# Attention and mixture-of-experts kernel: one transfer for the layernorm statistics, gate biases on GpSimd's queue, results read a tile sooner, four late stores on other queues or places

## The chip, the cores and the metric

The kernel runs on one core of a Trainium2 chip. The core has five engines that run at the same time: TensorE (PE, matrix products), VectorE (DVE), ScalarE (ACT), GpSimd (POOL) and SyncE (SP). SyncE, ScalarE and GpSimd each have a queue from which they issue transfers; 16 DMA engines, shared by all queues, move the data between the main memory (DRAM) and the on-chip memory (SBUF). Matrix products land in PSUM, which is read by VectorE and ScalarE.

The metric is the device time in microseconds (us). Three runs of the kernel before gave 610.34, 611.74 and 612.23; the median is 611.74. A profile shows one execution, with the start and length of each instruction and with what an engine waited for.

## The reference, cut to what matters

For each of B = 4 batches of 512 tokens with 512 features (1024 context rows), all in float32:

```python
# x: (4, 512, 512), ctx: (4, 1024, 512)
h = layernorm(x)
q, g = h @ Wq.T, sigmoid(h @ Wg.T + bg)
k, v = split(ctx @ Wkv.T)                  # 16 heads of 32
q, k = where(q > 0, q + 1, exp(q)), where(k > 0, k + 1, exp(k))
attn = (q @ (k.T @ v)) / (q @ sum(k) + 1e-6)   # per head
x = x + (attn * g) @ Wo.T
# two of eight experts for each token
h = layernorm(x)
w, sel = top_k(h @ Wr, 2); w = softmax(w)
x = x + sum_i w[i] * (h @ We[sel[i]] + be[sel[i]])
```

## The kernel before, in words

**Attention.** Context tiles of 128 rows (eight a batch) are loaded by `load_ctx` into three buffers (`cT`); `keys` and `values` multiply them by `wkv_sb` into PSUM (`pk`, `pv`), and `kv_add` adds the products of keys and values into `kvs`. `query` and `gate` multiply the transposed, normalized x (`xT`) by `wq_sb` and `wg_sb`; the gate's sigmoid (line 423) takes its bias from `bg_sb`. `products` and `attention_out` finish the attention. The program order on TensorE is kept, by `keep_in_program_order`. So is that of SyncE's loads, all of which go through `load` (line 102): a load that waits for a buffer holds back those behind it.

**The layernorm in front of the attention.** x is also loaded as `blocks` (`load_blocks`), in a layout in which 32 by 32 transposes on VectorE give `xT`. In that layout the rows of a token sit on other partitions than in the tiles on which the statistics are made. `layernorm_stats` makes mean and variance of four tiles of 128 tokens (into `mv`, four pairs a partition) and from the variance 1/sqrt (into `rstd`). `spread_moments` writes both to DRAM (`moments`), by GpSimd's queue, and reads them back four times, into 32 partitions each (`ln`). `normalized_T` uses `ln` as scalars. For batch 0 the order on SyncE's queue is: weights and x, the context tile 3, `wq`, `blocks`, `wr`, context tile 4, then for seven pieces a load of `bg_sb` and one of `wo_sb` in turn (lines 948 to 950), then context tiles 5 and 6. The biases are loaded as columns of single floats.

**The experts.** `choose` picks two experts for each token and `dispatch` scatters the tokens' rows into a DRAM buffer `stream`, sorted by expert (GpSimd's indirect DMAs). `run` goes over tiles of 128 rows of it. There are EARLY = 17 tiles that can be taken before the last batch is sorted, and then SURE = 18 late steps. At step j of `run`, SyncE issues the loads of tile j + 5 (four parts of `xg`, and `of` with the token numbers; line 765), TensorE multiplies tile j by its expert's weights (`pe`), VectorE adds the bias (`y`, line 814), GpSimd scatters y into `result` (line 818), and VectorE transposes tile j + 3 (line 782).

**Reading the results.** The output has 16 tiles of 128 tokens. `fetch` reads both choices of a tile from `result` (`y<-result`, 0.5 MB, line 889), `add` combines them with x on VectorE (line 902), and `store` writes the tile to the output (line 913). A read waits until as many scatters as its group in `READ` asks for have landed: 13 for tiles 0 to 3, 21 for 4 to 7, 26 for 8 and 9, 29 for 10 and 11, 33 for 12 and 13, all for 14 and 15. `begins` gives the late step after which the read of tiles 0 to 13 is placed; the add stands three steps later and the store one more, unless the read begins at step 14 (SURE - 4) or later: then add and store come after the loop. `queue_of` gives GpSimd's queue up to step 12 and ScalarE's after it. On each queue the order is that of the program. After the loop the reads of 14 and 15 go out on ScalarE's queue, then the adds and stores that are left; the store of tile 14 is on SyncE's queue, that of 15 on ScalarE's.

Of the kernel before, what the change touches and what calls it, by code (L numbers as in the profile page):

```python
# [9 lines left out]
F32 = mybir.dt.float32  # L10
I32 = mybir.dt.int32
U32 = mybir.dt.uint32
AF = mybir.ActivationFunctionType
ALU = mybir.AluOpType
# [3 lines left out]
P = 128  # L18
B, L, S, D = 4, 512, 1024, 512
E, F = 8, 512  # L20
HD = 32
NC = D // P
NT = L // P
# [16 lines left out]
SURE = LATE - 4  # L40
# [13 lines left out]
def xattn_moe_kernel(  # L54
# [14 lines left out]
    nc = tc.nc  # L69
# [10 lines left out]
    small = ctx.enter_context(tc.tile_pool(name="small", bufs=2))  # L80
    pmm = ctx.enter_context(tc.tile_pool(name="pmm", bufs=6, space=PSUM))
    pkv = ctx.enter_context(tc.tile_pool(name="pkv", bufs=1, space=PSUM))
    dram = ctx.enter_context(tc.tile_pool(name="dram", bufs=1, space=DRAM))
# [3 lines left out]
    result = dram.tile([NOWHERE + 2 * L, F], F32, name="result")  # L87


    moments = dram.tile([B, HD, NT, P // HD, 2], F32, name="moments")  # L90


    def matmul(**operands):
# [8 lines left out]
    def load(dst, src):  # L102
        latest["load"] = nc.sync.dma_start(out=dst, in_=src)  # L103
        tc.keep_in_program_order(latest["load"])
# [39 lines left out]
    bg_sb = wpool.tile([P, NC], F32, name="bg_sb")  # L144
# [17 lines left out]
    xs = {0: load_x(0)}  # L162

    turned = [(g, 0, g * HD, P - g * HD) for g in range(NC)]
# [17 lines left out]
    eps_sb = const.tile([P, 1], F32, name="eps_sb")  # L182
# [16 lines left out]
    for g in range(NC):  # L199
        r = slice(g * HD, (g + 1) * HD)  # L200
        for i in range(NC):
            o = (i + g) % NC
            nc.gpsimd.affine_select(
                out=spread[r, o, :], in_=spread[r, o, :], pattern=[[0, HD]],
# [49 lines left out]
    def layernorm_stats(tiles):  # L254
        mv = small.tile([P, NT, 2], F32, tag="mv", name="mv")
        for t in range(NT):
            st = small.tile([P, 6], F32, tag="st", name="st")
            nc.vector.bn_stats(st, tiles[t])
            nc.vector.bn_aggr(mv[:, t, :], st)
        rstd = small.tile([P, NT], F32, tag="rstd", name="rstd")  # L260
        nc.scalar.activation(rstd, mv[:, :, 1], AF.Sqrt, bias=eps_sb)
        nc.vector.reciprocal(rstd, rstd)
        return mv, rstd

    def normalize(dst, xt, t, mv, rstd):
        nc.vector.tensor_scalar(
            dst, xt, mv[:, t, 0:1], rstd[:, t : t + 1], ALU.subtract, ALU.mult
        )

    def transposed(dst, src):  # L270

# [4 lines left out]

    def spread_moments(b, tiles):

        mv, rstd = layernorm_stats(tiles)
        for k, of in enumerate((mv[:, :, 0], rstd)):  # L280
            nc.gpsimd.dma_start(
                out=moments[b, :, :, :, k].rearrange("t n j -> j t n"), in_=of
            )
        ln = small.tile([P, NT, P // HD, 2], F32, tag="ln", name="ln", bufs=1)
        for i in range(NC):
            nc.gpsimd.dma_start(
                out=ln[ts(i, HD)].rearrange("t n j k -> t (n j k)"),
                in_=moments[b].rearrange("t n j k -> t (n j k)"),
            )
        return ln  # L290

    def normalized_T(xT, t, blocks, ln):

        rows = blocks[:, ts(t, D)].rearrange("p (j f) -> p j f", f=P)
        with tc.issue_after(latest["map"].ins):
            for j in range(P // HD):
                nc.vector.tensor_scalar(
                    rows[:, j], rows[:, j], ln[:, t, j, 0:1], ln[:, t, j, 1:2],
                    ALU.subtract, ALU.mult,
                )  # L300
            nc.vector.transpose(
                xT[:, :, ts(t, P)].rearrange("p c (j t) -> p j c t", t=HD),
                rows.rearrange("p j (c f) -> p j c f", f=HD),
            )
# [41 lines left out]
    def kv_blocks(psum):  # L346
        for h in range(P // HD):
            r = slice(h * HD, (h + 1) * HD)
            nc.scalar.copy(h_kv[r], psum[r, :, r])
            nc.vector.tensor_copy(h_ks[r, :, h : h + 1], psum[r, :, P : P + 1])  # L350
# [23 lines left out]
    def kv_tiles(b, lo, hi, between=None, inside=None):  # L374
        for s in range(lo, hi):
            nxt = (b, s + 2) if s + 2 < NS else (b + 1, s + 2 - NS)
            if nxt[0] < B and nxt not in loaded_ctx:
                loaded_ctx.add(nxt)
                ctx_tiles[nxt] = load_ctx(*nxt)
            if b in (1, 2) and s % 2 == 0:  # L380
                e = (b - 1) * E // 2 + s // 2
                for i in range(NC):
                    load(we_sb[ts(i, HD), e], we_rows[e, i])
            for e in (s,) if b else (2 * (s - NS // 2), 2 * (s - NS // 2) + 1):
                if e >= 0:
                    set_empty(b, e)
            if s == 0:
                sums[b] = pkv.tile([P, NC, 2 * P], F32, tag="kvs", name="kvs")
            k = made.pop(s) if s in made else keys(b, s)
            if (b, s) == (0, 0):  # L390
                made[1] = keys(0, 1)
            if inside is not None and s == lo:
                inside()
            v = values(b, s)
            if s > 0:
                kv_add(sums[b], s - 1, *pending[b])
            pending[b] = k, v
            if between is not None:
                between(s - lo)
        if hi == NS:  # L400
            kv_add(sums[b], NS - 1, *pending[b])
# [121 lines left out]

    routed = {}

    def choose(b, mv, rstd):

        rows = []
        batch = work.tile([P, NT, ROW], F32, tag="row", name="rows", bufs=1)
        for t in range(NT):  # L530
            row = batch[:, t, :]
            normalize(row[:, 0:D], xs[b][t], t, mv, rstd)
            nc.gpsimd.tensor_copy(row[:, D : D + 1], home[:, b * NT + t : b * NT + t + 1])
            rows.append(row)

        xT = big.tile([P, NC, L], F32, tag="aT", name="x2T")
        for t in range(NT):
            transposed(xT[:, :, ts(t, P)], rows[t])
            yield

        ps = pmm.tile([P, L], F32, tag="mm", name="ps")
        for c in range(NC):
            matmul(
                out=ps[ts(c, HD), :],
                lhsT=wr_sb[:, c, :],
                rhs=xT[:, c, :],
                start=True,
                stop=True,
                tile_position=(0, c * HD),
            )  # L550
        share = work.tile([P, L], F32, tag="z", name="share")
        nc.scalar.copy(share, ps)
        yield
        pl = pmm.tile([P, NT, E], F32, tag="mm", name="pl")
        for t in range(NT):
            matmul(
                out=pl[:, t, :], lhsT=share[:, ts(t, P)], rhs=by_expert, start=True, stop=True
            )
        lg = small.tile([P, NT, E], F32, tag="lg", name="lg")
        nc.vector.tensor_copy(lg, pl)  # L560

        def largest(name):
            m = small.tile([P, NT, 1], F32, tag=f"m{name}", name=f"m{name}")
            hot = small.tile([P, NT, E], F32, tag=f"hot{name}", name=f"hot{name}")
            at = small.tile([P, NT, 1], F32, tag=f"at{name}", name=f"at{name}")
            nc.vector.tensor_reduce(m, lg, AX.X, ALU.max)
            nc.vector.tensor_tensor(hot, lg, m.to_broadcast([P, NT, E]), ALU.is_equal)
            nc.vector.tensor_tensor(hot, hot, rank, ALU.mult)
            nc.vector.tensor_reduce(at, hot, AX.X, ALU.max)
            nc.vector.tensor_tensor(hot, hot, at.to_broadcast([P, NT, E]), ALU.is_equal)  # L570
            return m, hot, at

        m1, hot1, first = largest("1")
        nc.vector.scalar_tensor_tensor(lg, hot1, -BIG, lg, ALU.mult, ALU.add)
        m2, hot2, _ = largest("2")

        routed[b] = rows, m1, hot1, first, m2, hot2
        yield
# [347 lines left out]
    def plan(step, *what):  # L926
        at_step.setdefault(min(step, SURE), []).append(what)

    def queue_of(step):
        return nc.gpsimd if step < SURE - 5 else nc.scalar  # L930

    begins = (-3, -2, -1, 0, 5, 6, 7, 8, 10, 11, 14, 15, SURE - 2, SURE - 2)
    for g, (lo, hi, most) in enumerate(READ):
        for t in range(lo, hi):
            plan(begins[t], fetch, t, most, queue_of(begins[t]), g)
    for t, begin in enumerate(begins):
        step = begin + (3 if begin < SURE - 4 else SURE)
        plan(step, add, t, gates if step < SURE else gates_end)
        plan(step + 1, store, t, queue_of(step + 1))

    def also(j):
        for what, *of in at_step.pop(j, []):
# [3 lines left out]
    xT = new_xT()  # L946
    kv_tiles(0, 0, 3)
    for g, a, b, n in turned:
        load(bg_sb[b : b + n, g : g + 1], bg[a : a + n, g : g + 1])
        load(wo_sb[b : b + n, g, :], wo[a : a + n, g, :])  # L950
    ln = spread_moments(0, xs[0])

# [2 lines left out]
            normalized_T(xT, t, blocks, ln)  # L955

    kv_tiles(0, 3, NS, between)
    kv_blocks(sums[0])
    for b in range(B):
        more = b + 1 < B  # L960
# [43 lines left out]
        if more:  # L1004
# [11 lines left out]
            ln = []  # L1016
# [4 lines left out]
            for _ in range(3):  # L1021
                next(early)
        attention_out(b, aT)
        choice = choose(b, *layernorm_stats(xs[b]))
        if more:

            def between(i):
# [133 lines left out]
```

## Time and profile before

| what | us |
|---|---|
| median of three runs | 611.74 |
| the profiled execution | 610.59 |
| its span, first to last instruction | 608.9 |
| TensorE busy | 576.7 |
| VectorE busy | 289.6 |
| GpSimd busy | 120.5 |
| ScalarE busy | 109.3 |

Instructions are named by line, engine, operation and "out<-in" with the program's names of tiles. `pk<-wkv_sb,cT` is a matmul of a context tile with the weights of the keys. "SPq", "ACTq" are transfers as they are issued on SyncE's and ScalarE's queues; "x4" stands for four in a row. In a line of the timeline the first number is the start and the second the length, in us; a bracket at the end gives how long the engine had been idle and what ended it. The row PEclk gives the granted clock of TensorE in 40 equal slices, in tenths of full speed (9 is 90% or more). The table by stretch gives start and end, the length, the busy time of PE, its weight loads, DVE, ACT and POOL with the number of instructions, and at the end the clock, the share of time in which the 16 DMA engines are busy (it can exceed 1, as packets overlap), and GB/s.

### The profile page before, as it was taken

To read this page: it belongs to the slowest core of one execution; us is meant where nothing else is said; L and a number is where in the kernel's file an instruction comes from. 1 tells how busy PE (TensorE), PEld (TensorE's weight loads), DVE (VectorE), ACT (ScalarE), POOL (GpSimd) and SP (SyncE) were. 2 spreads that over 40 slices of the span, in tenths; PEclk is the share of its full clock that TensorE was granted. 3 is DMA by queue.
4 is the path that set the end of the run, shared out by engine and by line. 5 is a ranking of instruction groups with operands and counts; after the bars stand their busy time and mean duration, and the time that the engine had idled before them with its cause. 6 is when DMAs were issued, how large, how long until landed. Compare 5 with 4: busy or idle time off the path is not lost.

```text
span 608.9 us, 6440 instructions
## 1 busy us (share of the span) xinstructions
PE 576.7 (95%) x1780; PEld 270.0 (44%) x1780; DVE 289.6 (48%) x732; ACT 109.3 (18%) x168; POOL 120.5 (20%) x289
## 2 busy tenths in 40 slices
PE   7989999999999999999999999999999999998950
PEld 3545544454555435445543454554344443443420
DVE  2215254354317443541564355128765579473863
ACT  1311241220313321122242121221300110000000
POOL 4230021000001510000061100003211237444630
PEclk9989999999999999999999999999999999999995
DMA  8979995374490698627338660952255444889866
GB/s 283 166 122 355 340 197 48 116 238 131 121 277 19 140 240 261 190 87 209 103 140 147 236 203 5 315 221 108 89 119 121 121 122 167 251 235 295 243 225 212
DMA packets 78933, 109.87 MB, mean 180 GB/s; under 512 B 13229, under 2 KB 39853, under 8 KB 78768
## 3 DMA queue, kind: packets, MB, share of 16 engines
q1 hardware_dynamic: 68112, 79.91, 49.0%
q0 software_dynamic: 8336, 24.29, 12.2%
q10 hardware_dynamic: 2448, 5.24, 2.6%
q8 instruction: 15, 0.25, 0.2%
q14 instruction: 22, 0.18, 0.1%
HBM read 50.19 MB, written 59.96 MB: 181 GB/s over the span
## 4 chain that ended last, share of the span: by engine, by line
PE 74%; DMA 9%; DVE 6%; SPq 4%; issue 4%; POOL 1%; DVEq 0%; ACTq 0%; POOLq 0%
PE pk L94 18%; PE pv L94 16%; PE pq L94 9%; PE po L94 9%; PE pg L94 7%; PE pe L94 5%; PE kvs L94 4%; DMA xg<-stream 4%; DMA cT<-in_cT_dram 3%; SPq L765 2%; SPq L103 1%; PE pn L94 1%; PE pt L97 1%; DMA result<-y,to 1%; DMA of<-stream 1%
## 5 line engine op out<-in xcount | busy, mean ns | idle before, releaser
L94 PE MATMUL pk<-wkv_sb,cT 128*128 128x512 f32 x256 | 119.4, 611 | 6.4 <-DMA cT<-in_cT_dram 6.4
L94 PE MATMUL pv<-wkv_sb,cT 128*128 128x512 f32 x256 | 115.2, 593 | 0.0
L250 DVE TENSOR_SCALAR ex<-pk 128x512 f32<-128x512 f32 x32 | 22.1, 692 | 135.1 <-PE pk L94 135.1
L94 PEld LDWEIGHTS pv<-wkv_sb,cT 128*128 128x128 f32 x256 | 48.4, 190 | 62.3 <-issue 59.8
L94 PEld LDWEIGHTS pk<-wkv_sb,cT 128*128 128x128 f32 x256 | 48.0, 196 | 60.9 <-issue 53.4
L94 PE MATMUL pe<-we_sb,xgT 128*128 x144 | 62.8, 594 | 3.9 <-DVE xgT L782 3.9
L94 PE MATMUL pe<-we_sb,turned_rows 128*128 x136 | 60.4, 596 | 1.9 <-DVE turned_rows L782 1.5
L94 PE MATMUL pg<-xT,wg_sb 128*128 128x512 f32 x128 | 56.7, 595 | 0.0
L94 PE MATMUL pq<-xT,wq_sb 128*128 128x512 f32 x128 | 56.6, 596 | 0.0
L94 PE MATMUL po<-wo_sb,aT 128*128 128x512 f32 x128 | 55.6, 592 | 0.0
L818 POOL DMA_INDIRECT result<-y,to x35 | 36.4, 1041 | 94.0 <-DVE y L814 91.3
L251 ACT ACTIVATE ex<-ex 128x512 f32<-128x512 f32 x48 | 30.2, 629 | 137.5 <-DVE ex L250 117.3
L330 POOL MEMSET v<- 128x4 f32 x32 | 3.3, 108 | 245.4 <-PE kvs L94 245.3
L94 PEld LDWEIGHTS pe<-we_sb,xgT 128*128 128x128 f32 x144 | 27.1, 190 | 39.4 <-issue 32.2
L624 POOL DMA_INDIRECT stream<-rows,slot x32 | 32.9, 1027 | 51.7 <-DVE acc L587 22.2
L94 PEld LDWEIGHTS kvs<-v,k 128*128 128x128 f32 x256 | 33.3, 191 | 16.0 <-issue 14.2
L94 PEld LDWEIGHTS pe<-we_sb,turned_rows 128*128 128x128 f32 x136 | 25.2, 190 | 34.0 <-issue 29.9
L94 PEld LDWEIGHTS pg<-xT,wg_sb 128*128 128x128 f32 x128 | 24.0, 190 | 32.1 <-issue 32.1
L94 PEld LDWEIGHTS po<-wo_sb,aT 128*128 128x128 f32 x128 | 24.1, 190 | 29.2 <-issue 28.7
L94 PEld LDWEIGHTS pq<-xT,wq_sb 128*128 128x128 f32 x128 | 23.8, 190 | 27.3 <-issue 27.3
L94 PE MATMUL kvs<-v,k 128*128 128x129 f32 x256 | 34.1, 275 | 0.0
L252 DVE SCALAR_TENSOR_TENSOR k<-pk,ex 128x512 f32<-128x512 f32 x32 | 22.1, 691 | 21.6 <-ACT ex L251 21.6
(183 smaller groups left out, 459.7 us busy)
## 6 DMA issues: line engine op xcount, KB each, us to landing
stream<-empty SPq DMA_DIRECT2D x24, 1028.0 KB
stream<-empty SPq DMA_DIRECT2D x8, 1285.0 KB
xg<-stream SPq DMA_DIRECT2D x140, 64.0 KB
we_sb<-in_we_dram SPq DMA_DIRECT2D x32, 256.0 KB
cT<-in_cT_dram SPq DMA_DIRECT2D x31, 256.0 KB
y<-result POOLq DMA_DIRECT2D x10, 512.0 KB
x<-in_x_dram SPq DMA_DIRECT2D x16, 256.0 KB
blocks<-in_x_dram SPq DMA_DIRECT2D x16, 256.0 KB
```

The source lines that it names most:

```text
L94: tc.keep_in_program_order(nc.tensor.matmul(**operands))
L97: tc.keep_in_program_order(nc.tensor.transpose(dst, src, ident))
L103: latest["load"] = nc.sync.dma_start(out=dst, in_=src)
L250: nc.vector.tensor_scalar(ex, src, 0.0, None, ALU.min)
L251: nc.scalar.activation(ex, ex, AF.Exp)
L252: latest["map"] = nc.vector.scalar_tensor_tensor(dst, src, 0.0, ex, ALU.max, ALU.add)
L330: nc.gpsimd.memset(v[:, :, P : P + 1], 1.0)
L624: put = nc.gpsimd.indirect_dma_start(out=stream, out_offset=bass.IndirectOffsetOnAxis(ap=slots[i][:, t, :], axis=0), in_=rows[t], in_offse ...
L765: load = nc.sync.dma_start(out=dst, in_=src)
L818: put = nc.gpsimd.indirect_dma_start(out=result, out_offset=bass.IndirectOffsetOnAxis(ap=home_i, axis=0), in_=y, in_offset=None, bounds_ch ...
```

## The change

Four edits go together.

- The statistics: `layernorm_stats` writes the reciprocal of the deviation over the variance in `mv`, so that mean and factor of a token lie side by side. `moments` and `ln` are laid out with the four tiles innermost, so that one DMA, with one piece of eight floats (32 bytes) a partition, takes the place of two with four single floats a partition each. The four reads back stay as they are in number and size.
- The gate biases: the seven loads of `bg_sb` move from SyncE's queue, where they stood between the seven loads of `wo_sb`, to GpSimd's queue, behind the work on the context tiles of batch 0.
- `begins`: the reads of tiles 4 to 9 are placed one step sooner, those of 10 and 11 two steps sooner. Tiles 10 and 11 thereby get their adds (steps 15, 16) and stores (16, 17) within the loop.
- `queue_of`: GpSimd's queue is used up to step 11. From step 12 on a read goes to ScalarE's queue; the stores of tiles 8 and 9 (steps 13, 14) go to SyncE's queue, those of 10 and 11 to ScalarE's.

```diff
-    moments = dram.tile([B, HD, NT, P // HD, 2], F32, name="moments")
+    moments = dram.tile([B, HD, P // HD, NT, 2], F32, name="moments")
...
-        rstd = small.tile([P, NT], F32, tag="rstd", name="rstd")
-        nc.scalar.activation(rstd, mv[:, :, 1], AF.Sqrt, bias=eps_sb)
-        nc.vector.reciprocal(rstd, rstd)
-        return mv, rstd
-
-    def normalize(dst, xt, t, mv, rstd):
-        nc.vector.tensor_scalar(
-            dst, xt, mv[:, t, 0:1], rstd[:, t : t + 1], ALU.subtract, ALU.mult
-        )
+        dev = small.tile([P, NT], F32, tag="rstd", name="dev")
+        nc.scalar.activation(dev, mv[:, :, 1], AF.Sqrt, bias=eps_sb)
+        nc.vector.reciprocal(mv[:, :, 1], dev)
+        return mv
+
+    def normalize(dst, xt, mv):
+        nc.vector.tensor_scalar(dst, xt, mv[:, 0:1], mv[:, 1:2], ALU.subtract, ALU.mult)
...
-        mv, rstd = layernorm_stats(tiles)
-        for k, of in enumerate((mv[:, :, 0], rstd)):
-            nc.gpsimd.dma_start(
-                out=moments[b, :, :, :, k].rearrange("t n j -> j t n"), in_=of
-            )
-        ln = small.tile([P, NT, P // HD, 2], F32, tag="ln", name="ln", bufs=1)
+        mv = layernorm_stats(tiles)
+        nc.gpsimd.dma_start(out=moments[b].rearrange("t j n k -> j t (n k)"), in_=mv)
+        ln = small.tile([P, P // HD, NT, 2], F32, tag="ln", name="ln", bufs=1)
         for i in range(NC):
             nc.gpsimd.dma_start(
-                out=ln[ts(i, HD)].rearrange("t n j k -> t (n j k)"),
-                in_=moments[b].rearrange("t n j k -> t (n j k)"),
+                out=ln[ts(i, HD)].rearrange("t j n k -> t (j n k)"),
+                in_=moments[b].rearrange("t j n k -> t (j n k)"),
             )
...
-                    rows[:, j], rows[:, j], ln[:, t, j, 0:1], ln[:, t, j, 1:2],
+                    rows[:, j], rows[:, j], ln[:, j, t, 0:1], ln[:, j, t, 1:2],
...
-    def queue_of(step):
-        return nc.gpsimd if step < SURE - 5 else nc.scalar
-
-    begins = (-3, -2, -1, 0, 5, 6, 7, 8, 10, 11, 14, 15, SURE - 2, SURE - 2)
+    def queue_of(step, behind=nc.scalar):
+        return nc.gpsimd if step < SURE - 6 else behind
+
+    begins = (-3, -2, -1, 0, 4, 5, 6, 7, 9, 10, 12, 13, SURE - 2, SURE - 2)
     for g, (lo, hi, most) in enumerate(READ):
         for t in range(lo, hi):
             plan(begins[t], fetch, t, most, queue_of(begins[t]), g)
     for t, begin in enumerate(begins):
         step = begin + (3 if begin < SURE - 4 else SURE)
         plan(step, add, t, gates if step < SURE else gates_end)
-        plan(step + 1, store, t, queue_of(step + 1))
+        plan(step + 1, store, t, queue_of(step + 1, nc.sync if step < SURE - 4 else nc.scalar))
...
     for g, a, b, n in turned:
-        load(bg_sb[b : b + n, g : g + 1], bg[a : a + n, g : g + 1])
         load(wo_sb[b : b + n, g, :], wo[a : a + n, g, :])
     ln = spread_moments(0, xs[0])
...
     kv_tiles(0, 3, NS, between)
+    for g, a, b, n in turned:
+        nc.gpsimd.dma_start(out=bg_sb[b : b + n, g : g + 1], in_=bg[a : a + n, g : g + 1])
     kv_blocks(sums[0])
```

More of the change, by code (lines that the diff above doesn't have):

```diff
@@ L524, in xattn_moe_kernel, with choose @@
     routed = {}
-    def choose(b, mv, rstd):
+    def choose(b, mv):
         rows = []
@@ L531, in choose @@
             row = batch[:, t, :]
-            normalize(row[:, 0:D], xs[b][t], t, mv, rstd)
+            normalize(row[:, 0:D], xs[b][t], mv[:, t])
             nc.gpsimd.tensor_copy(row[:, D : D + 1], home[:, b * NT + t : b * NT + t + 1])
@@ L1023, in xattn_moe_kernel @@
         attention_out(b, aT)
-        choice = choose(b, *layernorm_stats(xs[b]))
+        choice = choose(b, layernorm_stats(xs[b]))
         if more:
```

## The prediction

> **What bounds the kernel now.** I read the page first, then the chain of work that ended last, then the timeline of the queues around each place where the chain leaves TensorE, and last busy time and DMA rate in chosen stretches.
>
> ```profile
> span 608.9 us, 6440 instructions
> PE 576.7 (95%) x1780; PEld 270.0 (44%) x1780; DVE 289.6 (48%) x732; ACT 109.3 (18%) x168; POOL 120.5 (20%) x289
> PEclk9989999999999999999999999999999999999995
> ```
>
> TensorE is busy for 95% of the span, so only the 32 us in which it is not, and the stretches in which its clock falls, can be won. From 45 to 440 us every five-microsecond stretch has it busy throughout. What is left: 4.45 us until the first operands land, one hole near 38 us, waits that add up to some 6 us between 440 and 588, and the last 20 us, after its last matmul. The change touches the hole, the late loop (514 to 590) and the end.
>
> The hole, in the chain of the first 60 us (start, length, what):
>
> ```profile
> 26.61 12.30 DMA cT<-in_cT_dram
> ...
> 39.05 5.37 PE pk L94 x8
> ...
> 48.74 3.51 PE pk L94 x8
> ```
>
> The keys of context tile 4 wait for a load issued at 26.61 that lands at 38.91. TensorE had finished at 36.9 (36.00 plus 0.89 for the last kvs group), so it stands 2.1 us. The same eight matmuls take 3.43 us elsewhere and 5.37 here.
>
> ```profile
> 18.24 1.74 POOL L281 DMA_DIRECT2D moments<-mv  x1 [9.63 <-DVE mv L259]
> 20.12 1.53 POOL L281 DMA_DIRECT2D moments<-rstd  x1
> 36.06 2.03 POOL L286 DMA_DIRECT2D ln<-moments  x4 [14.26 <-DMA moments<-rstd]
> 42.64 0.58 SPq L103 DMA_DIRECT2D bg_sb<-in_bg_dram  x1
> 43.79 0.84 SPq L103 DMA_DIRECT2D cT<-in_cT_dram  x2
> ```
>
> The statistics go out in two DMAs, and 14.3 us pass before GpSimd may read them back. On SyncE, context tile 5 is issued at 43.79, behind seven bias and seven wo loads.
>
> In the table by stretch the last three numbers are the clock, the DMA share and GB/s:
>
> ```profile
> 26.00:30.00 4.00, 4.00 (x17) 2.23 (x16) 0.69 (x1) 2.28 (x3) 0.00 (x0) 1.00 1.44 57
> 40.00:41.00 1.00, 1.00 (x2) 0.34 (x1) 0.00 (x0) 0.00 (x0) 0.95 (x5) 0.50 0.47 110
> 78.00:82.00 4.00, 4.00 (x11) 1.72 (x10) 3.85 (x9) 1.18 (x3) 0.00 (x0) 1.00 1.19 172
> 214.00:216.00 2.00, 2.00 (x25) 0.49 (x24) 0.56 (x1) 0.69 (x1) 0.00 (x0) 1.00 0.56 41
> 216.00:218.00 2.00, 2.00 (x12) 0.87 (x5) 2.00 (x5) 0.00 (x0) 0.00 (x0) 1.00 0.98 221
> 598.00:606.00 8.00, 0.00 (x0) 0.00 (x0) 3.01 (x4) 0.00 (x0) 0.00 (x0) 0.50 0.95 321
> ```
>
> The blocks loads (512-byte runs) move at 172 and 221 GB/s when alone (78 to 82, 216 to 218), and at 57 and 41 GB/s while the statistics of a batch are on their way out (26 to 30, 214 to 216). At 40 us the clock is half.
>
> The end:
>
> ```profile
> 577.28 0.36 ACTq L889 DMA_DIRECT2D y<-result  x1
> 585.47 3.70 PE L94 MATMUL pe<-we_sb,xgT 128*128 x8 [1.70 <-DVE xgT L782]
> 590.47 5.94 DMA result<-y,to
> 596.95 5.62 DMA y<-result
> 597.49 7.01 ACTq L913 DMA_DIRECT2D out_dram<-y  x5
> ```
>
> The last scatter takes 5.94 us to land, the read of tiles 14 and 15 then 5.62, while ScalarE's queue issues five stores beside it.
>
> **The change, part by part.**
>
> *Statistics.* Before, two DMAs of 512 four-byte elements each a batch (128 partitions by 4); after, one of 128 runs of 32 bytes. The reciprocal writes into mv instead of rstd, 4 values a partition, 0.17 us as before; the readers differ in stride alone. GpSimd loses one issue of 1.77 us a batch, hidden anyway: no normalization (line 297) waited for ln (0.0 idle before all 64), and no kvs matmul shows idle time of its own. The gain is on the DMA queue. In the first batch the blocks loads run from 24 to 36 us, and the context load is behind them on the same queue. At 172 GB/s their 1.05 MB take 6.1 us, so they would end at 30.1, 5.9 earlier, and the load would land at 33.0 instead of 38.9; with an eighth of the slowdown left (128 runs for 1024) at 33.7. TensorE needs it by 36.9. A third of the relief closes the hole. With the hole goes the half clock, which lasts from about 39.7 to 43.0 and costs 5.37 - 3.43 = 1.94 us. So 44.42 becomes 36.9 + 3.43 = 40.3: 4.1 us. Ends: nothing, if the load stays late, and 4.1. I take 4.1, as the slow stretch is there in the other batches too and ends when the statistics are out.
>
> The Trainium skill, "DMA: Bandwidth & Descriptors", section "Why a DMA increments its semaphore by 16 and not by 1", says that a transfer uses the largest number of engines up to 16 that divides the slowest dimension of both sides; here these are 4 and 128, so it would use 4, before and after. An estimate by that: 32 runs on an engine instead of 128 elements leave a quarter of the slowdown, 1.5 us, and the load lands at 34.5; the sum stays, the margin falls from 3.2 to 2.4 us.
>
> *Gate biases.* Seven issues leave SyncE: 0.45 + 0.34 + 0.56 + 0.58 + 0.42 + 1.35 + 0.58 = 4.3 us. Context tile 5 goes out by 39.5 instead of 43.79, earlier still if the queue drains faster. It is needed at 44.6 instead of 48.7 once the hole is closed, and took at most 4.9 us to land, so 44.4 at the latest: without this part the hole would move to tile 5. On GpSimd the seven come after the memset of 64.5 and before that of 72.3, both moved 4 us ahead. The nearest rows, 0.52 us (ln) and 1.77 us (statistics), give 3.6 to 12.4 us of issue, and up to 14.3 us for the landing. GpSimd's next work with a reader is the statistics of batch 1 at 82.6; the first sigmoid needs the biases at 90.3. Even the upper end, 64.6 + 12.4 + 14.3 = 91.3, would reach it by only 1 us, with six PSUM buffers between it and TensorE. I take nothing.
>
> *Results a tile sooner.* The reads of tiles 4 to 9 move one step ahead, 10 and 11 two, and the adds and early stores with them. On GpSimd the read of tile 4 comes behind scatter 4 and waits for scatter 3 (issued 543.23). Scatters land within about 5.7 us (scatter 11, issued 571.62, releases the read on ScalarE at 577.28), so until 549, against 549.96 now; scatter 5 behind it slips from 548.0 to some 549.6. The y buffers behind it are five, and nothing on TensorE waits. The reads of 4 to 7 then go out within 549 to 555 instead of 550 to 559.4, so one read of 0.52 MB more (1.5 us at the 346 GB/s of 555 to 560) meets the row loads whose lateness costs TensorE 1.6 us at 562.9: 0 to 1.5 us lost. Reads 8 and 9 and three stores leave the stretch from 570 to 577, which runs full, while read 11 enters it behind read 10 (577.7 instead of 582.5). The wait of 1.70 us before tile 17 may go (-1.7) or grow by one read (+1.5). Together -1.7 to +3.0; I take 0, as a read moves out of each full stretch for about each that moves in. VectorE does the adds of 10 and 11 (4 x 0.75 us) before y16 and y17 instead of after; its idle 0.99 us and the missing add of tile 9 there cover most of it.
>
> *Stores.* Those of 8 and 9 go to SyncE at steps 13 and 14; its row loads end with step 12, so nothing queues behind them. Those of 10 and 11 go out on ScalarE behind reads 12 and 13, at about 591.5 instead of 597.5. From 598 to 606 the DMA engines are 95% busy with 2.57 MB, which is the last two reads (1.05) and six stores (1.57). Two stores less are 0.52 MB at 321 GB/s, 1.6 us; part of it comes back if they slow the last scatter (592 to 596 has share 0.80 and 0.62, so 1.2 us free). Ends 0 and 1.6; I take 1.2.
>
> Sum: 610.59 - 4.1 - 0 - 0 - 1.2 = 605.3 for the profiled execution (span 608.9 and 1.7 around it). That execution lies 1.15 under the median of the runs, so the median becomes 606.4.
>
> **The rivals.**
>
> *The clock drop is not the hole's.* For: after the last matmul (588.9) the clock falls only near 592.8, 3.9 us later, and the idle 1.6 us at 561.3 costs no clock. Against: 39.7 is just behind the only hole of 2 us before the end. Then 2.1 us instead of 4.1 are won: 608.4. The Trainium skill, "TensorE: Matmul & The Clock Gate", section "Why this matters for your kernels", asks only for no idle gaps above about 3 us, by which the 2.1 us should not have dropped the clock. The row at 40 us has 0.50 all the same.
>
> *The context load stays late.* It would if the blocks loads are slow by themselves beside the wq and wr loads. For: wq moves at 210 GB/s before them. Against: 221 GB/s at 216 us, right behind the statistics. Then only the end is won: 610.5.
>
> *Slower: the reads meet the row loads.* TensorE waits for each row tile, and eight reads move onto them. If each delays one row load by its own 1.5 us with nothing overlapped, 12 us are lost: 606.4 + 12 = 618. It decides for slower from 7.2 us on (five reads), since 5.3 are won. Half the price, 6 us, gives 612.4 and no change. Against: the DMA engines have free share in 540 to 545 (0.60) and 565 to 570 (0.67).
>
> *A milder late loop* loses the 3.0 us of its upper bound: 609.4.
>
> **How the numbers follow.** Forecast 0.62 (606.4; 604.2 to 608 by the bounds of the late loop and the end), clock 0.12 (608.4), load late 0.10 (610.5), mild late loop 0.06 (609.4), slower 0.10. Within 0.3%, about what a measurement of this kernel can tell from no change, is 609.9 to 613.6. Faster: 0.62 + 0.12 + 0.04 of the mild case = 0.78; same 0.10 + 0.02 = 0.12; slower 0.10. The range 604.0 to 611.0 leaves out the slower case and a little of the forecast's low end.
>
> **What would show it.** Statistics: the wait of ln for moments falls from 14.3 to under 8 us in the first batch, and the rate from 26 to 30 is above 120 GB/s. Hole: no wait of pk for cT beyond tile 0, the second PEclk slices at 9, the first pq matmul at about 69 instead of 73.1. Biases: aT's sigmoid waits for pg alone. End: last matmul near 585, and from there to the end 18.8 us instead of 20. Wrong it would be if cT still ends the wait at tile 4 or 5, or if xgT's waits for DMA grow beyond the 18.0 us of now.

## The result, and the profile after

The changed kernel takes 605.29 us (median; runs from 603.6 to 605.91) against 611.04 (610.26 to 612.23) for the kernel before on the same chip. The ratio is 0.9906, with an interval of [0.9877, 0.9935]. The forecast was 606.4 with a range from 604.0 to 611.0. The profiled execution took 605.65, against 610.59 before.

The page of the kernel after:

```profile
span 604.0 us, 6430 instructions
PE 575.1 (95%) x1780; PEld 269.3 (45%) x1780; DVE 289.9 (48%) x732; ACT 109.2 (18%) x168; POOL 114.4 (19%) x292
PEclk9999999999999999999999999999999999999995
```

TensorE's busy time is 1.6 us shorter, with the same 1780 matmuls: the slice of reduced clock near the start is gone. The rest of the 4.9 us by which the span shrank is idle time.

TensorE's timeline of the kernel after, at the place where the hole was (start, length, what):

```profile
36.46 1.05 PE L94 MATMUL kvs<-v,k 128*128 128x129 f32 x8
37.35 3.60 PE L94 MATMUL pk<-wkv_sb,cT 128*128 128x512 f32 x8
40.79 3.60 PE L94 MATMUL pv<-wkv_sb,cT 128*128 128x512 f32 x8
```

The keys of context tile 4 follow the kvs group at once and run at full clock. (A matmul's length in this view includes its last, overlapping part; the step from one start to the next is 3.44.) I measure the hole from here on as the time from the start of this kvs group to the start of the next pv, less the 4.33 us that it takes here. Before, that was 44.26 - 36.00 - 4.33 = 3.9 us, and now 0.

The statistics on GpSimd's queue, the kernel after:

```profile
8.53 3.92 POOL L953 DMA_DIRECT2D bg_sb<-in_bg_dram  x7
20.55 0.75 POOL L278 DMA_DIRECT2D moments<-mv  x1 [8.10 <-DVE mv L262]
30.36 1.99 POOL L281 DMA_DIRECT2D ln<-moments  x4 [8.11 <-DMA moments<-mv]
```

Its second number before the bracket is the time to issue: 0.75 us in place of 1.74 + 1.53. The read back waits 8.1 us for the write to land, and waited 14.3. The seven bias loads are at 8.53, ahead of the statistics, although they stand behind them in the program: on this queue the order is not that of the program throughout.

The table by stretch of the kernel after (last three numbers: clock, DMA share, GB/s):

```profile
26.00:30.00 4.00, 4.00 (x16) 2.23 (x15) 0.85 (x2) 2.50 (x3) 0.00 (x0) 1.00 1.22 167
40.00:41.00 1.00, 1.00 (x4) 0.50 (x3) 0.01 (x1) 0.00 (x0) 0.00 (x0) 1.00 1.05 401
214.00:216.00 2.00, 2.00 (x6) 0.76 (x4) 1.57 (x3) 0.00 (x0) 0.00 (x0) 1.00 1.06 221
592.00:600.00 8.00, 0.00 (x0) 0.00 (x0) 3.61 (x5) 0.00 (x0) 0.00 (x0) 0.50 0.73 229
```

From 26 to 30 the loads move 167 GB/s instead of 57. The last row is the stretch that lies as far behind the last matmul as the one from 598 to 606 did before: the DMA engines are busy for 73% of it, with 229 GB/s, where it was 95% and 321. Whether that shortened the end is another matter, taken up below.

SyncE's queue in the kernel after: the load of tile 4 goes out at 26.20 (before 26.61) and those of tiles 5 and 6 together from 33.86 (before 43.79).

```profile
26.20 0.38 SPq L103 DMA_DIRECT2D cT<-in_cT_dram  x1
...
33.86 3.15 SPq L103 DMA_DIRECT2D cT<-in_cT_dram  x2
```

The end of the kernel after, first TensorE's timeline, then the last scatter and the stores behind it, then the chain that ended last:

```profile
554.93 20.87 PE L94 MATMUL pe<-we_sb,xgT 128*128 x48 [1.03 <-DVE xgT L777]
575.95 7.13 PE L94 MATMUL pe<-we_sb,xgT 128*128 x16 [0.16 <-DVE xgT L777]
```

```profile
584.40 0.98 POOL L813 DMA_INDIRECT result<-y,to  x1 [0.73 <-DVE gates_end L1083]
...
585.94 1.13 ACTq L908 DMA_DIRECT2D out_dram<-y  x2
```

```profile
592.47 0.36 ACTq L884
...
592.87 5.51 DMA y<-result
...
599.19 0.75 DVE y L897
```

The last matmul ends at 583.1, and the span 20.9 us later. In the same view of the kernel before it is 589.2 (585.47 + 3.70) and 19.7; the prediction took 588.9 and 20. The read of tile 14 goes out at 592.47, that of tile 15 right behind it, and the latter takes 5.51 us to land (before 5.62).

### The profile page after: what moved, and what is told of

Its sections match the earlier page's. It is cut to its first block, busy times and chain, and to the rows that moved or that the text cites. A ratio compares the mean times of both kernels' runs of the same rounds, so it can differ in the third digit from the quotient of the medians.

```text
span 604.0 us, 6430 instructions
## 1 busy us (share of the span) xinstructions
PE 575.1 (95%) x1780; PEld 269.3 (45%) x1780; DVE 289.9 (48%) x732; ACT 109.2 (18%) x168; POOL 114.4 (19%) x292
## 3 DMA queue, kind: packets, MB, share of 16 engines
q0 software_dynamic: 8304, 24.25, 11.4%
## 5 line engine op out<-in xcount | busy, mean ns | idle before, releaser
L94 PE MATMUL pk<-wkv_sb,cT 128*128 128x512 f32 x256 | 118.0, 605 | 4.5 <-DMA cT<-in_cT_dram 4.5
L813 POOL DMA_INDIRECT result<-y,to x35 | 36.9, 1053 | 90.8 <-DVE y L809 87.5
L619 POOL DMA_INDIRECT stream<-rows,slot x32 | 32.8, 1024 | 51.7 <-DVE acc L582 22.2
```

The source lines that it names most:

```text
L94: tc.keep_in_program_order(nc.tensor.matmul(**operands))
L619: put = nc.gpsimd.indirect_dma_start(out=stream, out_offset=bass.IndirectOffsetOnAxis(ap=slots[i][:, t, :], axis=0), in_=rows[t], in_offse ...
L813: put = nc.gpsimd.indirect_dma_start(out=result, out_offset=bass.IndirectOffsetOnAxis(ap=home_i, axis=0), in_=y, in_offset=None, bounds_ch ...
```

## The experiments

The theory going in was that of the prediction: the statistics' small writes hold up the DMA queues, with them the load of context tile 4, and so make the hole and the drop of the clock; the other three edits are worth little. The rivals were that the gain comes from the bias loads that left SyncE's queue, or from the late loop and the end; that the clock drop has another cause; and that the size of the pieces is not what matters about the statistics.

The first four kernels shared one set of 21 runs of the kernel before (median 610.23), the other four another of 17 (609.89). Gains are given by the ratio.

### The statistics alone

The kernel before, with all that the change does to `moments`, `mv` and `ln`, and nothing else of it.

```diff
...
-        for k, of in enumerate((mv[:, :, 0], rstd)):
-            nc.gpsimd.dma_start(
-                out=moments[b, :, :, :, k].rearrange("t n j -> j t n"), in_=of
-            )
+        nc.gpsimd.dma_start(out=moments[b].rearrange("t j n k -> j t (n k)"), in_=mv)
...
```

> The statistics in one transfer alone; biases on SyncE's queue and the reading of results as before. Theory (the single floats hold up the blocks loads): the context load of tile 4 lands before 36.9 us and TensorE does not stand there; the rate from 26 to 30 us is above 120 GB/s; the half clock near 40 us is gone. With the seven bias loads still in front of it, context tile 5 goes out 4.3 us later than in the changed kernel (33.9 there), so at 38.2, and lands by 43.1, before it is needed at 45.1: 3.5 to 4 us won, 607.1 to 607.6. Rival 1, as the prediction put it: without the move of the biases the hole goes to tile 5, and only 0 to 1 us is won. Rival 2: the blocks loads are slow by themselves, the hole stays, 611.0.

Measured: 605.15 us, ratio 0.9918 [0.9891, 0.9944], so 5.0 us less than before (3.4 to 6.7 by the interval). That is 2 us under the range that the theory gave, and not told apart from the 5.75 of the whole change. TensorE's timeline and SyncE's queue of this kernel:

```profile
35.52 1.05 PE L94 MATMUL kvs<-v,k 128*128 128x129 f32 x8
36.41 3.60 PE L94 MATMUL pk<-wkv_sb,cT 128*128 128x512 f32 x8
...
44.17 3.60 PE L94 MATMUL pk<-wkv_sb,cT 128*128 128x512 f32 x8
```

```profile
38.96 0.84 SPq L103 DMA_DIRECT2D cT<-in_cT_dram  x2
```

The hole is closed at tile 4 and does not move to tile 5, although the bias loads are still on SyncE's queue: with the blocks loads faster, the queue reaches tile 5 at 38.96 instead of 43.79, and tile 5 has no wait at 44.17. No gain of the rest of the change can be seen beside it.

### The bias loads alone

The kernel before, with this edit.

```diff
     for g, a, b, n in turned:
-        load(bg_sb[b : b + n, g : g + 1], bg[a : a + n, g : g + 1])
         load(wo_sb[b : b + n, g, :], wo[a : a + n, g, :])
...
+    for g, a, b, n in turned:
+        nc.gpsimd.dma_start(out=bg_sb[b : b + n, g : g + 1], in_=bg[a : a + n, g : g + 1])
```

> The gate biases on GpSimd's queue alone. Theory: the load of context tile 4 was issued before the first bias load, so the hole of 2.1 us and the half clock behind it stay; 610.5 to 611.5, no change. Rival: the 512 single floats of the biases on the DMA engines were what held the context load up, the hole closes, 607.5.

Measured: 610.77 us, ratio 1.0013 [0.9981, 1.0045]: no change. The hole stays, in TensorE's timeline:

```profile
35.73 1.05 PE L94 MATMUL kvs<-v,k 128*128 128x129 f32 x8
39.91 6.50 PE L94 MATMUL pk<-wkv_sb,cT 128*128 128x512 f32 x8 [3.12 <-DMA cT<-in_cT_dram]
46.25 3.60 PE L94 MATMUL pv<-wkv_sb,cT 128*128 128x512 f32 x8
```

By the measure above it costs 46.25 - 35.73 - 4.33 = 6.2 us here, against 3.9 in the profile before. The bias loads stood behind the load of tile 4, in front of that of tile 5, so their move does not close it. The load of tile 4 was issued at 32.66 here, 6 us later than before, and TensorE got it only 0.9 us later: here its landing is not set by when it is issued. The clock is half from 38.8 on, as the table by stretch shows (0.90 in the row from 38 to 39 means that the clock was half for a fifth of it):

```profile
38.00:39.00 1.00, 0.00 (x0) 0.00 (x0) 0.00 (x0) 0.00 (x0) 0.91 (x5) 0.90 1.06 249
40.00:41.00 1.00, 1.00 (x2) 0.48 (x3) 0.00 (x0) 0.00 (x0) 0.00 (x0) 0.50 0.90 208
45.00:46.00 1.00, 1.00 (x3) 0.52 (x2) 0.00 (x0) 0.00 (x0) 0.00 (x0) 0.69 1.06 395
```

### The late loop and the stores alone

The kernel before, with the change's `begins`, `queue_of` and line of the stores.

```diff
-    begins = (-3, -2, -1, 0, 5, 6, 7, 8, 10, 11, 14, 15, SURE - 2, SURE - 2)
+    begins = (-3, -2, -1, 0, 4, 5, 6, 7, 9, 10, 12, 13, SURE - 2, SURE - 2)
...
-        plan(step + 1, store, t, queue_of(step + 1))
+        plan(step + 1, store, t, queue_of(step + 1, nc.sync if step < SURE - 4 else nc.scalar))
```

> The sooner reads and the stores alone; statistics and biases as before. Theory (what the two profiles show for the late part is due to these edits): the waits of TensorE for row tiles after 520 us fall from 3.9 to about 1.2 us, and the time from the last matmul to the end grows from 19.7 to about 20.9: 1.5 us won, 609.5. Rival: the late loop's waits are a matter of where the transfers happen to fall in an execution, and not of these edits: then the waits stay near 3.9 us and the end costs 1.2 us more, 612.2.

Measured: 609.94 us, ratio 1.0012 [0.9976, 1.0048]: no change, in ten runs between 606.86 and 614.99. TensorE's timeline:

```profile
40.37 5.06 PE L94 MATMUL pk<-wkv_sb,cT 128*128 128x512 f32 x8 [3.08 <-DMA cT<-in_cT_dram]
...
559.21 20.96 PE L94 MATMUL pe<-we_sb,xgT 128*128 x48 [1.35 <-DVE xgT L782]
581.51 7.13 PE L94 MATMUL pe<-we_sb,xgT 128*128 x16 [1.33 <-DVE xgT L782]
```

The hole is there (4.7 us). In the late loop the new order leaves waits of 1.35 and 1.33 us, 2.7 together, where the kernel after, with the same late loop, had 1.2. From the last matmul (588.6) to the end of the span it is 20.4 us, where the profile before has 19.7. Neither the sooner reads nor the stores can be seen in the time.

### Statistics and bias loads, old late loop

The changed kernel, with `begins`, `queue_of` and the line of the stores as they were before. This and the four that follow are edits to the changed kernel.

```diff
-    begins = (-3, -2, -1, 0, 4, 5, 6, 7, 9, 10, 12, 13, SURE - 2, SURE - 2)
+    begins = (-3, -2, -1, 0, 5, 6, 7, 8, 10, 11, 14, 15, SURE - 2, SURE - 2)
...
-        plan(step + 1, store, t, queue_of(step + 1, nc.sync if step < SURE - 4 else nc.scalar))
+        plan(step + 1, store, t, queue_of(step + 1))
```

> Statistics and biases changed, reading and storing of results as before. Theory: the hole is closed (3.5 to 4 us), the late loop and the end are those of the kernel before, with 3.9 us of waits for row tiles and 19.7 us behind the last matmul: 607.2 to 607.6. Rival: the late loop's gain comes from what the statistics take off the DMA engines or from the shift of the whole, then it is here too: 604.7.

Measured: 605.03 us, ratio 0.9914 [0.9884, 0.9943]. Without the two late edits the kernel is as fast as with them (0.9906). The number is that of the rival rather than of the theory. Whether the waits in the late loop get shorter with the statistics, as the rival has it, stays open: for xgT they are 3.9, 1.1 and 2.7 us in the three profiles with the old statistics and 0.3 to 3.2 us in the six without a hole. The lines of TensorE's timeline:

```profile
37.26 3.60 PE L94 MATMUL pk<-wkv_sb,cT 128*128 128x512 f32 x8
...
558.98 24.30 PE L94 MATMUL pe<-we_sb,xgT 128*128 x56 [1.96 <-DVE xgT L777]
```

No hole; a late wait of 1.96 us; 20.9 us from the last matmul to the end.

### One transfer of single floats

Here the layout of `moments` keeps mean and factor in one transfer, but in 1024 pieces of one float, to part the number of transfers from the size of the pieces. `ln` and its readers follow the layout.

```diff
-    moments = dram.tile([B, HD, P // HD, NT, 2], F32, name="moments")
+    moments = dram.tile([B, HD, NT, 2, P // HD], F32, name="moments")
...
-        nc.gpsimd.dma_start(out=moments[b].rearrange("t j n k -> j t (n k)"), in_=mv)
+        nc.gpsimd.dma_start(out=moments[b].rearrange("t n k j -> j t (n k)"), in_=mv.rearrange("p n k -> p (n k)"))
...
```

> The changed kernel, with the statistics still in one transfer, but laid out in DRAM so that it writes 1024 single floats again. Theory (the number of pieces holds the DMA engines up): the wait of ln in batch 0 is back above 12 us, the blocks loads run at 40 to 110 GB/s while it lasts, TensorE stands 2 to 3 us at tile 4 with the half clock behind it, and the time is 4 to 6 us above the changed kernel: 609.3 to 611.3. Rival: it was the second transfer, with its own issue and landing; then one transfer of single floats leaves the hole closed, 605.2.

Measured: 614.18 us, ratio 1.0072 [1.0046, 1.0099]: some 4.4 us slower than before, and about 3 above the theory's range. GpSimd's queue:

```profile
21.16 2.09 POOL L278 DMA_DIRECT2D moments<-mv  x1 [8.70 <-DVE mv L262]
42.88 2.00 POOL L281 DMA_DIRECT2D ln<-moments  x4 [19.51 <-DMA moments<-mv]
```

The table by stretch ahead of the hole, and TensorE's timeline at the hole, of this kernel:

```profile
30.00:34.00 4.00, 4.00 (x13) 1.90 (x12) 0.18 (x1) 0.16 (x1) 0.00 (x0) 1.00 0.83 60
34.00:38.00 4.00, 4.00 (x16) 2.19 (x14) 1.21 (x2) 1.21 (x2) 0.00 (x0) 1.00 0.53 30
```

```profile
44.45 5.56 PE L94 MATMUL pk<-wkv_sb,cT 128*128 128x512 f32 x8 [6.34 <-DMA cT<-in_cT_dram]
```

The write goes out at 21.16 and has landed by 42.88. From 26 to 30 the rate is still 181 GB/s, from 30 to 38 it falls to 60 and 30, TensorE stands for 6.3 us at tile 4, and the hole costs 49.85 - 37.05 - 4.33 = 8.5 us. So it is the pieces that hold up the loads, and one transfer by itself is no gain at all: 1024 pieces in one are worse than twice 512. By what the pieces hold them up is not shown: the share of the DMA engines is 1.44 in the slow stretch of the kernel before (26 to 30) and 0.53 in the slowest one here.

### Two transfers of 16-byte pieces

```diff
-        nc.gpsimd.dma_start(out=moments[b].rearrange("t j n k -> j t (n k)"), in_=mv)
+        for half in (ts(0, NT // 2), ts(1, NT // 2)):
+            nc.gpsimd.dma_start(
+                out=moments[b, :, :, half].rearrange("t j n k -> j t n k"), in_=mv[:, half, :]
+            )
```

> The changed kernel, with the statistics in two transfers of two tiles each: 256 pieces of 16 bytes. Theory (pieces): a quarter of the old number, so the hole stays closed, ln waits 8 to 10 us, 605.2. Rival (two transfers cost): the hole is back, 609.3 to 611.3.

Measured: 606.48 us, ratio 0.9944 [0.9923, 0.9965]. GpSimd's queue:

```profile
29.50 2.00 POOL L284 DMA_DIRECT2D ln<-moments  x4 [8.26 <-DMA moments<-mv]
```

The wait is that of the change (8.1) and the hole is closed in the profiled execution (0 by the measure). So a second transfer does not open the hole where the pieces are 128 each. The median lies 1.2 to 2 us above those of the other kernels without a hole. The profiled execution is the one of 606.48 itself, 0.8 us longer than that of the change, and has 2.1 us of waits for xgT in the late loop against 1.2: here it is not the hole that costs. Whether the hole comes back in other executions stays open.

### The late stores on SyncE's queue

```diff
-        plan(step + 1, store, t, queue_of(step + 1, nc.sync if step < SURE - 4 else nc.scalar))
+        plan(step + 1, store, t, queue_of(step + 1, nc.sync))
```

> The changed kernel, with the stores of tiles 10 and 11 on SyncE's queue as well, where they need not wait behind the reads of 12 and 13. Theory (the stores issued at 585.9 in the changed kernel are in the way of the last scatter, which took 8.1 us to release its reader against 6.1 before): they go out at about 581 and 584, the last scatter lands in about 6 us, and 1 to 2 us are won: 603.3 to 604.3. Rival: the landing time of the last scatter varies by itself, and nothing is won: 605.3.

Measured: 604.71 us, ratio 0.9919 [0.9898, 0.994]: not told apart from the change. From the issue of the last scatter to that of the read of tile 14 it is 6.5 us, as the theory had it, but from there to the end 12.4 us instead of 11.5, and from the last matmul to the end 20.4 us. Moving two more stores off ScalarE's queue doesn't shorten the end either.

### The write spread over its pieces another way

`moments` is laid out so that the transfer's 128 pieces make one contiguous block with 128 as its outermost size, instead of 4 by 32. The reads back follow the layout, with four pieces of 32 bytes a partition instead of one of 128.

```diff
-    moments = dram.tile([B, HD, P // HD, NT, 2], F32, name="moments")
+    moments = dram.tile([B, P // HD, HD, NT, 2], F32, name="moments")
...
-        nc.gpsimd.dma_start(out=moments[b].rearrange("t j n k -> j t (n k)"), in_=mv)
+        nc.gpsimd.dma_start(out=moments[b].rearrange("j t n k -> (j t) (n k)"), in_=mv)
...
```

> The changed kernel, with moments laid out so that the one transfer of statistics writes 128 pieces in one row after the other, as [128, 8] on both sides; the reads back take four pieces of 32 bytes a partition instead of one of 128. By the Trainium skill (DMA: Bandwidth & Descriptors, section Why a DMA increments its semaphore by 16 and not by 1) it would be spread over 16 DMA engines instead of 4. If that matters, the wait of ln for moments (8.1 us in batch 0, 7.7 in batch 1) falls by 1 us or more. The theory of the hole expects no difference in time either way, as ln is not waited for: 605.2.

Measured: 604.52 us, ratio 0.9912 [0.9885, 0.994], the same as the change. From GpSimd's queue and from TensorE's timeline:

```profile
29.40 2.20 POOL L281 DMA_DIRECT2D ln<-moments  x4 [7.02 <-DMA moments<-mv]
```

```profile
560.88 24.46 PE L94 MATMUL pe<-we_sb,xgT 128*128 x56 [2.58 <-DVE xgT L777]
```

The wait for the moments is 7.0 us in batch 0, against 8.1; in batch 1 it is 7.79 against 7.75, in batch 2 2.30 against 1.95, in batch 3 2.30 against 2.35. There is no clear gain in laying them out so.

The Trainium skill, "DMA: Bandwidth & Descriptors", section "Why a DMA increments its semaphore by 16 and not by 1", gives 16 engines to this write and 4 to those of the change and of the kernel with 1024 pieces. An estimate by it: the last two differ by 32 and 256 pieces an engine and by 11.4 us in the wait, so 0.05 us a piece; with 8 pieces an engine the wait would be 1.2 us shorter. Batch 0 (1.1 shorter) agrees and the other three (none shorter by more than 0.05) do not, so no run here decides whether the rule holds for it.

## Why the prediction was right, and where it was not

**The hole: right, and probably a little too small.** The statistics alone take 5.0 us off the runs where the step said 4.1, which still lies within the interval (3.4 to 6.7). That number was the cost of the hole in one execution, and its cost differs: 3.9, 6.2 and 4.7 us in the three profiles of kernels with the old statistics, 4.9 in the mean. The term of the sum should have been a range. The mechanism as told holds link by link: the pieces (1024 of them reopen the hole and widen it), the rate (57 to 167 GB/s), the load (tile 4 no longer waited for), the clock (1.00 at 40 us). The granted clock that is on record for every run fits a hole of changing size: 0.979 to 0.988 in the 21 runs of the kernel before, with 0.988 in the fastest (603.74), and 0.985 to 0.988 in the five runs with the statistics alone. That the hole was short or missing in the fastest runs is not shown; no trace of them was kept.

**The clock drop is the hole's.** Half clock near 40 us shows in the four profiles with a hole (before, bias loads alone, late part alone, 1024 pieces) and in none of the six without. That rival has fallen. (What was said for it was misread a little: by finer rows the clock at the end falls near 592.6, 3.4 us after the last matmul's end at 589.2.) The same comparison settles the rival of a load that is slow by itself.

**The bias loads: nothing, as said, but for two wrong claims.** "Without this part the hole would move to tile 5" failed: the step left the issue of tile 5 at its old time, 43.79, or 4.3 us sooner without the biases' own issues, while the whole queue behind the blocks loads moves ahead when those speed up. In the kernel with the statistics alone tile 5 went out at 38.96. And the place of the seven loads on GpSimd's queue was misread: they are issued at 8.53, not behind the memset of 64.5, which makes them safer still (0.56 us to issue each).

**Sooner reads: nothing, as said.** TensorE's waits for xgT in the late loop add up, in the four profiles of the old order, to 3.9 (before), 1.1 (statistics alone), 1.1 (bias loads alone) and 2.0 us (old late loop): 2.0 in the mean. In the new order they are 1.2 (after), 2.7 (late part alone), 1.9, 2.1, 3.2 and 0.3 us (1024 pieces, two transfers, spread write, late stores on SyncE's queue): 1.9 in the mean. The 2.7 us less between the two profiles that are shown, before and after, lie within this scatter. The same goes for the slower rival: the reads do not hold up the row loads to any amount that can be seen, and VectorE's wait for xg is 16.3 us in all, not above 18.0. One profile says little here: in the eight of the experiments it goes from 13.9 to 23.4 us, and the longest is one of the old order. The group of VectorE's transposes, from the table of groups of the kernel after (busy time and mean ns of one, then the idle time before them and what ended it):

```profile
L777 DVE STREAM_TRANSPOSE xgT<-xg 128x512 f32<-128x512 f32 x18 | 12.7, 707 | 17.7 <-DMA xg<-stream 16.3 <-issue 1.4
```

**Stores: wrong, 0 instead of 1.2.** The step priced the end by the bytes that the DMA engines have to move from 598 on, since they were 95% busy there. In the same stretch behind the last matmul they are at 73% now, and the end is as long: from the last matmul to the end of the span 19.7, 20.1, 19.4 and 20.9 us in the old order (20.0 in the mean), 20.9, 20.4, 19.5, 21.1 and 19.1 in the new (20.2), 20.4 with all late stores on SyncE's queue. Its parts show where the bytes went. From the issue of the read of tile 14 to the end of the span it is 11.9 to 12.4 us in the old order (12.1 in the mean of four) and 11.3 to 11.9 in the new (11.5 in the mean of five): with two stores less beside the last reads, some 0.6 us are won. But from the issue of the last scatter to that of this read it is 6.1 to 6.6 us in the old order (6.4 in the mean) and 6.6 to 8.1 in the new (7.2), so some 0.8 us come back. Two stores now stand right behind the last scatter (585.94 in the kernel after). The step named such a return, and allowed for 0.4 us of it. That the stores are what delays the scatter is argued, not shown: with them on SyncE's queue the first part is 6.5 us, but the second is 12.4. The read of tile 15 got no faster: 5.4 to 5.7 us until it has landed, in both orders (before, after and the first four experiments). "18.8 us from there to the end" failed with this step.

**The sum.** The hole was put some 0.9 us too small and the stores 1.2 us too large. That the two nearly cancel is luck: 5.3 us were forecast and 5.75 measured (4.0 to 7.5 by the interval of the ratio). Of the 1.1 us by which the median lies under the forecast, 0.7 are the kernel before, whose median over four runs is 611.04 instead of 611.74. The profiled executions differ by 610.59 - 605.65 = 4.9 us: 3.9 less for the hole, 2.7 less in the late waits, 0.5 more at the start (its first 16 matmuls took 9.7 us instead of 9.3) and 1.2 more at the end. The last three lie within the scatter of the profiles, so the total alone would have seemed to confirm steps that the runs refute.

Of the signs named beforehand, these came true: the rate above 120 GB/s, no wait of pk for cT beyond tile 0, PEclk at 9 in all slices but the last, the first pq matmul near 69 (69.43), the sigmoid waiting for pg alone, the last matmul near 585 (583.1). The wait of ln just missed "under 8" with 8.1.

## What to carry to other kernels

A transfer of many tiny pieces is paid for by the others: price it by what the loads beside it lose, and look for it in the rate of the stretch in which it is on its way, not on the engine that issued it. Where DMA engines are busy at the end of a kernel, price also what the moved transfers do in their new place: here about as much came back in front of the last read as was won behind it. Before reading a gain of an edit out of two profiles, run it alone: in this kernel the waits in the late loop add up to 1.1 to 3.9 us in four profiles of the same order.

## What the runs showed of the hardware that was not expected

- The wait for the write of the statistics grows with the pieces of one transfer, and the loads beside it slow down with it: 8.1 us with 128 pieces, 12.6 to 14.3 with twice 512, 19.5 with 1024 (batch 0). In batch 1 it is 7.75, 13.5 and 20.0 us (after, before, 1024 pieces); in batch 2, 1.95, 10.8 and 17.3; in batch 3, 2.35, 13.3 and 20.6.
- A wait of little over 2 us can halve the clock. Before, TensorE stood from 36.9 to 39.05, and the clock fell at 39.6; but waits of 1.96 and 2.58 us in the late loops above cost none. The half clock then lasts 3.4 us (before; late part alone) or twice that, 6.8 us (bias loads alone, from 38.8 to 45.6; 1024 pieces), by the shares in the table by stretch. That is why a wait that was 1.1 us longer (36.62 to 39.91, against 36.89 to 39.05) cost 2.3 us more with the bias loads alone than before. The Trainium skill, "TensorE: Matmul & The Clock Gate", section "What's actually happening", tells of a window of about 3.4 us that runs freely and of the low clock after an idle one. The steps of 3.4 us agree; that the window must be idle as a whole does not, since TensorE stood for only 2.1 us in the kernel before. That it depends on how the wait falls into the windows would fit all these rows, and is argued, not shown.
- The kernel before scatters more than was seen at first: from 603.74 to 613.38 in 21 runs, where the first three lay within 2 us.
